# Grouped seven-product attention for layer 1, and layer 2's value projection moved behind its attention, in a six-layer graph network

## The chip, the core and the metric

The kernel runs on one NeuronCore of a Trainium2 chip. TensorE (PE) multiplies matrices, VectorE (DVE) and ScalarE (ACT) do elementwise work, GpSimd (POOL) does little here, and SyncE (SP) issues nearly all transfers. The metric is the device time of one execution in microseconds, and lower is better. All tensors that matter are float32.

## What is computed

The input is a matrix `x` of 3327 rows by 256 features and a 0/1 adjacency matrix of 3327 by 3327. Four residual layers follow one another, each `x = layernorm(x + layer(x))`. The last of them holds three graph attention layers, so the kernel counts six: "0", "1", "2", "3a", "3b", "3c". Each has masked attention over all rows:

```python
# layer 1
h = x @ W
e = leaky_relu((h @ a1)[:, None] + (h @ a2)[None, :])
att = softmax(where(adj > 0, e, -1e12), axis=1)
x = layernorm(x + elu(att @ h))
# layer 2
q, k, v = x @ Wq.T + bq, x @ Wk.T + bk, x @ Wv.T + bv
att = softmax(where(adj > 0, q @ k.T / 16, -9e15), axis=-1)
x = layernorm(x + elu(att @ v))
```

Layers 3a to 3c have the form of layer 1, with the layer norm after 3c alone. Because a row of `att` sums to one, `att @ (x @ W + b)` equals `(att @ x) @ W + b`: a projection can stand before the attention or behind it.

## The kernel before

Rows are padded to 3328, that is 26 tiles of 128 rows (`NT`) and 7 blocks (`NB`): blocks 0 to 5 have four tiles (512 query rows), block 6 has two. The main loop walks over `(L, b, j)`: layer, query block, key tile. For each step an attention weight tile `e` (128 keys by 512 queries) is made some steps ahead, and PE multiplies it with the value tile `V[L.i % 2][j]`, adding up in four PSUM banks `pos`. `V[0]` and `V[1]` take turns as a layer's input and output.

**Two ways to multiply.** In the plain way (the matmul at L1693), a step issues four matmuls of 128 by 128 by 257, the 257th column being the row sum. In the other way (`products`, L940), two key tiles make a pair, and seven products of the Strassen-Winograd kind replace eight. With 512 queries they are 14 matmuls with 128 or 129 columns to a pair, in place of 8 with 257. This needs sums of weights (`s1` to `s4`) and sums of values (`t1` to `t4`). The value sums are made once for each pair by `combine` (four DVE instructions of 128x128), stored in DRAM (`t_d`), and read back for each block by `fetch_tsum` into three buffers named `tsums`. Weight sums come from `sums` for one pair, or from `quad_sums` for a quad of four key tiles at once: there the weights lie in `QUADS`, which share their storage with `FT`.

**Who uses which.** `strassen(L, b)` says it: layer 0 in blocks 1 to 5, layer 2 in every block, 3a to 3c in blocks 0 to 5. Layer 1 is plain everywhere. Quads are used by 3a to 3c (`deep(L)`).

**`FT`** is the store of turned (transposed) feature tiles: layer 0's keys and queries, then layer 2's keys, which are layer 1's output turned. From layer 3a on nobody needs it, and it serves as `QUADS`.

**Layer 2's scores.** `pair_weights` (L638 to L678) makes the weights of two key tiles with seven products of its own (L650), from grouped keys (`ksum`, made by `sum_keys`, some kept and the others made anew in each block) and grouped queries (`gsum`). It is a generator; `products` steps it, so that score matmuls and attention matmuls lie mixed in PE's queue. Its products share two PSUM banks of three, and each is overwritten only after ACT or DVE has read what was in it.

**The end of a block** is `finish(L, b, pos)`, also a generator; the main loop advances it one step per `j` during the next block. It joins the seven products (`joined`, DVE, L972 to L984), normalises (ACT, L1188 or L1190), turns the result, projects it, applies elu, adds the residual, takes the layer norm (`bn_stats`, `rsqrt`), writes the output tile, and makes what the next layer needs. `turn` (L987) splits a block's floats into 16-bit planes (two ACT copies, L994), transposes them with one DMA (SP, L997), and joins the planes again with two copies (L1004, by DVE or ACT). In layer 1 it is done twice: for the attention's result before the projection (`projected4`, seven products, L1058, in blocks 0 to 4; L1247 in blocks 5 and 6), and for the output, into `FT[b]`. Then the value projection of layer 2 (`pv`, L1330) writes `x @ Wv + bv` into `V[0]`, and the output itself goes to DRAM (`x_d["2"]`), from where layer 2 reads it back as its residual. In layer 2 nothing is turned: the attention's result goes straight to elu.

The order of the work on an engine is not that of the source. A scheduler goes through the instructions in the source's order as a priority and issues those whose inputs and buffers are free in its own reckoning of time; each engine then runs its queue in that fixed order. Of the pools, `x4k` has two buffers (turned planes, `pT4`, `tsum`, layer 2's queries `gT`), `stage` four, `e` nine, `a` four, and the small PSUM banks three.

Of the kernel before, what the change touches and what calls it, by code (L numbers as in the profile page):

```python
# [33 lines left out]
def gnn_stack(ctx: ExitStack, tc: tile.TileContext, a: dict, N: int, out: bass.AP):  # L34
# [58 lines left out]
    for k in range(4):  # L93
# [21 lines left out]
        for k in ("0", "2", "3a", "3b", "3c")  # L115
    }
    x_d = {
        k: [dram.tile([P, D], F32, name=f"x{k}_d{t}") for t in range(NT)]
        for k in ("2", "3c")
    }  # L120
# [457 lines left out]
    def sum_queries(b):  # L578
# [23 lines left out]
        12: "w_l2_wvt",  # L602
    }

    KSTEPS = {4: 5, 6: 7, 8: 8, 11: 10, 14: 1, 16: 2, 18: 4, NT + 14: 11, NT + 16: 12}
# [99 lines left out]
    class Gat:  # L705
        def __init__(self, key):
            self.last = key == "3c"
            self.quads = ("3a", "3b", "3c").index(key) + 1 if key != "1" else 0
            self.k = w.get("k_" + key)
            self.row = w["row_" + key]  # L710
            self.sd = cols.tile([P, 2, NT], F32, tag="sd", name="sd")
            self.th = cols.tile([P, NT], F32, tag="th", name="th")
            self.rh = cols.tile([P, NT], F32, tag="rh", name="rh")
            self.nrh = cols.tile([P, NT], F32, tag="nrh", name="nrh")
            self.u = {}
# [69 lines left out]
        def weights(self, b, j):  # L785
# [9 lines left out]
            if self.quads and b < NB - 1:  # L795
                e = quad(self.quads, b, j)[:, j % 4, :]
            elif self.last and b == NB - 1:
                e = V[0][j]
            else:
                e = work.tile([P, CH], F32, tag="e", name="e", bufs=9)  # L800
# [15 lines left out]
    def strassen(L, b):  # L816
        if L.key == "0":
            return 0 < b < NB - 1
        if deep(L):
            return b < NB - 1  # L820
        return L.key == "2"

    def deep(L):
        return L.i > 2

# [5 lines left out]
    def combine(key, p, v, e=None):  # L831
# [4 lines left out]
        if (key, p) in kept or key == "0":  # L836
# [150 lines left out]
    def turn(x4, n, out, steps=3, copy=nc.vector.tensor_copy):  # L987

        half = "p k (n t) -> p t k n"
# [10 lines left out]
        trv = tr[:, : 4 * n, :].rearrange("p (k t h) i -> p t k h i", t=2, h=2)  # L1002
# [3 lines left out]

    def early(L, b):
        return deep(L) and b < NB - 2

    def turn_steps(L, b):  # L1010

        if L.key == "1":
            return 5 if b == NB - 2 else 3
# [10 lines left out]

    def sum_weights(wt):
        b11, b12, b21, b22 = (wt[:, h, o * H : (o + 1) * H] for h in range(2) for o in range(2))
        t1, t2, t3, t4 = wsum
        nc.vector.tensor_tensor(t1, b12, b11, ALU.subtract)
        nc.vector.tensor_tensor(t3, b22, b12, ALU.subtract)
        nc.vector.tensor_tensor(t2, b22, t1, ALU.subtract)  # L1030
        nc.vector.tensor_tensor(t4, t2, b21, ALU.subtract)

    def projected4(pT4, wt, c4):

        add, sub = ALU.add, ALU.subtract
        av = pT4.rearrange("p (a k) h q -> p a k h q", k=2)
        a11, a12, a21, a22 = (av[:, :, k, h, :] for k in range(2) for h in range(2))
        s3, s1, s2, s4 = (
            x[:, i, :].rearrange("p (a q) -> p a q", a=2)
            for x in two_slots("psums")  # L1040
            for i in range(2)
        )
        nc.vector.tensor_tensor(s3, a11, a21, sub)
        nc.vector.tensor_tensor(s1, a21, a22, add)
        nc.vector.tensor_tensor(s2, s1, a11, sub)
        nc.vector.tensor_tensor(s4, a12, s2, sub)
        yield
        b11, b12, b21, b22 = (wt[:, h, o * H : (o + 1) * H] for h in range(2) for o in range(2))
        t1, t2, t3, t4 = wsum
        cv = c4.rearrange("p (a k) (o f) -> p a k o f", k=2, o=2)  # L1050
        c11, c12, c21, c22 = (cv[:, :, k, o, :] for k in range(2) for o in range(2))

        def two(*pairs):

            pm = bank("pproj")
            for i, (l, r) in enumerate(pairs):
                for k in range(2):
                    nc.tensor.matmul(  # L1058
                        pm[:, (2 * i + k) * P : (2 * i + k + 1) * P],
                        l[:, k, :],  # L1060
                        r,
                        start=True,
                        stop=True,
                    )
            v = pm.rearrange("p (i a f) -> p i a f", i=2, a=2)
            return v[:, 0], v[:, 1]

        m1, m2 = two((a11, b11), (a12, b21))
        m6, m7 = two((s2, t2), (s3, t3))
        yield  # L1070
        nc.scalar.copy(c22, m1)
        nc.vector.tensor_tensor(c11, c22, m2, add)
        nc.vector.tensor_tensor(c22, c22, m6, add)
        nc.vector.tensor_tensor(c21, c22, m7, add)
        m5, m4 = two((s1, t1), (a22, t4))
        yield
        nc.vector.tensor_tensor(c12, c22, m5, add)
        nc.vector.tensor_tensor(c22, c21, m5, add)
        nc.vector.tensor_tensor(c21, c21, m4, sub)
        m3, _ = two((s4, b22))  # L1080
        yield
        nc.vector.tensor_tensor(c12, c12, m3, add)
# [23 lines left out]
    def finish(L, b, pos):  # L1106
# [76 lines left out]
        else:  # L1183
# [23 lines left out]
            if L.key in x_d:  # L1207
                x4 = work.tile([P, 4, D], F32, tag="stage", name="x4", bufs=4)
                xr = [x4[:, k, :] for k in range(4)]
                for k, t in enumerate(ts_):  # L1210
                    nc.sync.dma_start(xr[k], x_d[L.key][t])
# [5 lines left out]
            if L.key != "2":  # L1217
                pT4 = work.tile([P, 4, 2, P], F32, tag="x4k", name="pT4", bufs=2)
                yield from turn(
                    p4,  # L1220
                    n,
                    lambda t: pT4[:, :n].bitcast(U16).rearrange(
                        "p k h (i t) -> p t k h i", t=2
                    )[:, t],
                    turn_steps(L, b),
                    nc.scalar.copy if early(L, b) else nc.vector.tensor_copy,
                )
                if early(L, b):
                    yield
                    yield  # L1230
                pTs = {k: pT4[:, k] for k in range(n)}
                if L.key == "1" and b < NB - 2:
                    c4 = work.tile([P, 4, D], F32, tag="x4k", name="c4", bufs=2)
                    yield from projected4(pT4, w[L.w], c4)

            def projected(k):


                if L.key == "2":
                    src = p4[:, k, :]  # L1240
                elif L.key == "1" and b < NB - 2:
                    src = c4[:, k, :]
                else:
                    pm = bank("pproj")
                    pT = pTs.pop(k)
                    for h in range(2):
                        nc.tensor.matmul(  # L1247
                            pm[:, :D],
                            pT[:, h, :],
                            w[L.w][:, h, :],  # L1250
                            start=(h == 0),
                            stop=(h == 1),
                        )
                    src = pm[:, :D]
# [22 lines left out]
            for p in range(n + 2):  # L1277
                if p >= 2:
                    activated(p - 2)
                    if b == NB - 2 or early(L, b):  # L1280
# [7 lines left out]
        if not L.hidden:  # L1288
# [8 lines left out]
            else:  # L1297
                dsts = [nxt[t][:, :D] for t in ts_]
            for k, t in enumerate(ts_):
                nc.vector.tensor_scalar(  # L1300
                    dsts[k],
                    ys[k],
                    st[:, k, 0:1],
                    r[:, k : k + 1],
                    ALU.subtract,
                    ALU.mult,
                )
# [3 lines left out]
                elif L.key in ("1", "2"):  # L1311
                    nc.sync.dma_start(x_d["2" if L.key == "1" else "3c"][t], dsts[k])
# [4 lines left out]
            yield  # L1317
            if L.key == "1":
                yield from turn(
                    o4,  # L1320
                    n,
                    lambda t: FT[b].bitcast(U16).rearrange(
                        "p h (k i t) -> p t k h i", k=4, t=2
                    )[:, t, :n],
                    4 if b == NB - 2 else 3,
                )
                for k, t in enumerate(ts_):
                    pm = bank("pv")
                    for h in range(2):
                        nc.tensor.matmul(  # L1330
                            pm[:, :D],
                            FT[b][:, h, k * P : (k + 1) * P],
                            w["v"][:, h, :],
                            start=(h == 0),
                            stop=(h == 1),
                        )
                    nc.vector.tensor_tensor(nxt[t][:, :D], pm[:, :D], w["bv"], ALU.add)
                    if k % 2:
                        yield
                        if b < NB - 1:  # L1340
                            combine("2", t // 2, nxt)
                dsts = [nxt[t][:, :D] for t in ts_]
# [491 lines left out]
```

## Time and profile before

| | |
|---|---|
| median of 3 runs (lowest to highest) | 2261.28 us (2260.6 to 2264.51) |
| profiled execution | 2261.39 us, its span 2259.3 us |
| granted PE clock in it | 0.998 |
| PE busy | 2232.9 us (99%) |
| DVE busy | 1960.8 us (87%) |
| ACT busy | 1324.9 us (59%) |

The span is the time from the first to the last instruction; 2.1 us lie around it. "Busy" is the union of the time of an engine's instructions. A float32 matmul appears as two records on PE. From the starts of the main matmuls, layer 1's blocks begin at 467, 513, 565, 617, 669, 721 and 773 us, layer 2's at 807, 904, 988, 1072, 1156, 1239 and 1318 us, and those of 3a at 1359, 1405, 1451, 1496, 1540, 1584 and 1628 us.

### The profile page before, as it was taken

The page shows a single profiled execution, that of the slowest core. Times are in us where ns is not written, and L with a number is a line of the kernel's source. Part 1 is how long each engine was busy: PE and PEld are TensorE (multiplying, and loading weights), DVE is VectorE, ACT ScalarE, POOL GpSimd, SP SyncE. Part 2 cuts the span into 40 slices and gives each one's busy share as a digit, 9 for nine tenths or more (in the row PEclk, how much of TensorE's full clock was granted, in tenths as well). Part 3 has the DMA queues.
Part 4 walks back from the last instruction along what each step waited for, and adds up shares of the span by engine and source line. Part 5 has one row for each costly group of instructions (what it writes and reads, how often), then busy time and mean ns, then how long its engine had stood idle before and what let it go on. Part 6 is the DMA issues. An engine that isn't in the chain of part 4 may idle for free. (4 is left out here: it accounts for less than half of the span.)

```text
span 2259.3 us, 42140 instructions
## 1 busy us (share of the span) xinstructions
PE 2232.9 (99%) x15333; PEld 2026.2 (90%) x15333; DVE 1960.8 (87%) x5346; ACT 1324.9 (59%) x2259; POOL 78.6 (3%) x236
## 2 busy tenths in 40 slices
PE   9999999999999999999999999999999999999997
PEld 7788887888888879999999999999999999999997
DVE  7789999967667778988988889999898999899997
ACT  4677777775545534444454436766665765666663
POOL 0000001000000000000000000000000000000000
PEclk9999999999999999999999999999999999999999
DMA  8655665522332232223232244656535556355542
GB/s 279 197 177 171 195 193 190 177 90 68 92 82 55 68 87 78 66 92 92 57 97 76 76 143 151 157 146 167 143 114 157 152 144 169 101 168 162 153 121 56
DMA packets 191972, 291.41 MB, mean 129 GB/s; under 512 B 81054, under 2 KB 111253, under 8 KB 187157
## 3 DMA queue, kind: packets, MB, share of 16 engines
q1 hardware_dynamic: 185732, 283.22, 42.6%
q0 software_dynamic: 5760, 5.25, 1.5%
q8 instruction: 121, 1.98, 0.4%
q14 instruction: 87, 0.70, 0.1%
q10 hardware_dynamic: 272, 0.26, 0.0%
HBM read 228.21 MB, written 38.44 MB: 118 GB/s over the span
## 5 line engine op out<-in xcount | busy, mean ns | idle before, releaser
L788 ACT ACTIVATE re<-u,nrh,th 128x512 f32<-128x512 f32 (+1 forms) x728 | 534.0, 777 | 289.3 <-DVE e L801 147.1
L1693 PE MATMUL po<-v,e 128*128 128x257 f32 x1872 | 422.6, 381 | 0.7 <-ACT p L1190 0.6
L1693 PEld LDWEIGHTS po<-v,e 128*128 128x128 f32 x1872 | 352.6, 190 | 60.7 <-issue 9.8
L940 PE MATMUL po<-tsums,qsum 128*128 128x128 f32 (+1 forms) x2520 | 351.1, 275 | 0.9 <-DMA tsums<-t3b_d 0.5
L801 DVE SCALAR_TENSOR_TENSOR ft<-re,rh,mask 128x512 f32<-128x512 f32 x468 | 338.6, 742 | 1.9 <-ACT re L788 1.9
L940 PE MATMUL po<-tsums,ssum 128*128 128x128 f32 (+1 forms) x2082 | 316.9, 275 | 5.5 <-DMA tsums<-t3a_d 2.0
L940 PEld LDWEIGHTS po<-tsums,qsum 128*128 128x128 f32 x2520 | 315.4, 192 | 1.8 <-DMA tsums<-t3b_d 0.7
L940 PEld LDWEIGHTS po<-tsums,ssum 128*128 128x128 f32 x2082 | 286.6, 192 | 20.7 <-issue 5.0
L940 PE MATMUL po<-v,ft 128*128 128x129 f32 x1872 | 285.7, 275 | 1.0 <-DVE ft L801 0.9
L940 PEld LDWEIGHTS po<-v,ft 128*128 128x128 f32 x1872 | 251.6, 192 | 5.7 <-DVE ft L801 1.8
L940 PEld LDWEIGHTS po<-v,e 128*128 128x128 f32 x1196 | 170.2, 191 | 35.9 <-issue 23.7
L524 ACT ACTIVATE ex<-ps,rq 128x512 f32<-128x512 f32 (+1 forms) x183 | 118.9, 652 | 114.8 <-PE ps L511 111.9
L940 PE MATMUL po<-v,e 128*128 128x129 f32 x1196 | 183.3, 275 | 0.0
L801 DVE SCALAR_TENSOR_TENSOR e<-re,rh,mask 128x512 f32<-128x512 f32 (+1 forms) x234 | 148.3, 655 | 37.3 <-PE po L1693 22.5
L496 DVE SCALAR_TENSOR_TENSOR e<-ex,mask 128x512 f32<-128x512 f32 (+1 forms) x182 | 118.1, 649 | 61.0 <-ACT ex L673 30.6
L511 PE MATMUL ps<-ft 128*128 128x512 f32 (+1 forms) x364 | 166.9, 564 | 0.0
L525 DVE SCALAR_TENSOR_TENSOR e<-ex,mask 128x512 f32<-128x512 f32 (+1 forms) x183 | 116.6, 643 | 32.2 <-ACT ex L524 31.8
L940 PE MATMUL po<-tsums,ft 128*128 128x128 f32 x936 | 143.3, 275 | 0.0
L940 PE MATMUL po<-v,qsum 128*128 128x128 f32 x840 | 128.2, 275 | 0.0
L940 PEld LDWEIGHTS po<-tsums,ft 128*128 128x128 f32 x936 | 123.6, 192 | 0.1
L467 DVE CUSTOM_DVE_ANT_0 acc<-acc,stage 128x1024 uint16<-128x1024 uint16 (+1 forms) x168 | 108.6, 646 | 12.2 <-DMA stage<-in_adj_a 9.2
L650 PE MATMUL ps<-gsums,ksum 128*128 128x256 f32 x408 | 111.3, 380 | 0.0
(348 smaller groups left out, 3659.9 us busy)
## 6 DMA issues: line engine op xcount, KB each, us to landing
mask<-mask_d SPq DMA_DIRECT2D x30, 1664.0 KB
stage<-in_adj_a SPq DMA_DIRECT2D x78, 512.0 KB
tsums<-t_d SPq DMA_DIRECT2D x152, 256.5 KB
tsums<-t3a_d SPq DMA_DIRECT2D x77, 256.5 KB
tsums<-t3b_d SPq DMA_DIRECT2D x77, 256.5 KB
tsums<-t3c_d SPq DMA_DIRECT2D x77, 256.5 KB
mask_d<-mask SPq DMA_DIRECT2D x6, 1664.0 KB
u<-s_d SPq DMA_DIRECT2D x24, 256.0 KB
```

Of the source, the lines that this page charges most:

```text
L467: nc.vector.tensor_tensor(acc, acc, st[:, h * wd : (h + 1) * wd], ALU.add)
L496: nc.vector.scalar_tensor_tensor(e[:, :wd], t_[:, :wd], 0.0, mask(b, j), ALU.add, ALU.mult)
L511: nc.tensor.matmul(ps[:, :wd], FT[j // 4][:, 0, (j % 4) * P : (j % 4 + 1) * P], FT[b][:, 1, :wd], start=True, stop=True,)
L524: nc.scalar.activation(t_[:, c], ps[:, c], AF.Exp, scale=rq[:, j : j + 1])
L525: nc.vector.scalar_tensor_tensor(e[:, c], t_[:, c], 0.0, mask(b, j)[:, c], ALU.add, ALU.mult)
L650: nc.tensor.matmul(out, l, r, start=first, stop=True, skip_group_check=True)
L788: nc.scalar.activation(t_[:, :wd], self.u[b][:, :wd], AF.Relu, bias=self.nrh[:, j : j + 1], scale=self.th[:, j : j + 1],)
L801: nc.vector.scalar_tensor_tensor(e[:, :wd], t_[:, :wd], self.rh[:, j : j + 1], mask(b, j), ALU.add, ALU.mult,)
L940: nc.tensor.matmul(o, x, y, start=(p == 0 and g not in banks[:i]), stop=(p == NT // 2 - 1 and g not in banks[i + 1 :]),)
L1693: nc.tensor.matmul(pos[k], e[:, k * P : (k + 1) * P], V[L.i % 2][i], start=(i == 0), stop=(i == NT - 1),)
```

## The change

Layer 1 multiplies by seven products in blocks 1 to 5, with its weights in the quads of `FT`'s storage. So its turned output can't lie in `FT` while the layer runs: for blocks 0 to 4 it goes to DRAM (`tr_d`) and is fetched again in block 6 (`turned_again`), where ACT writes it to `FT`. Layer 1's value sums are made by `combine("1", ...)` in steps of layer 0's block 6 and of layer 1's blocks 0 and 1. `V[0]` now gets layer 1's output itself, by a transfer from the normalised tile, not the projected values; the output's turning and the steps behind it run in a second queue of generators (`tail`). The normalisation of layer 1 goes from DVE to ACT (`eased`). Its projection is the same for all blocks: eight matmuls at four tiles, not seven products. Layer 2's `finish` turns the attention's result and projects it with `Wv`, and DVE adds `bv`. Its residual is read from `V[0]`, and the grouped keys of pair 12 are no longer kept.

```diff
-        if L.key == "0":
+        if L.key in ("0", "1"):
             return 0 < b < NB - 1
-        if deep(L):
-            return b < NB - 1
-        return L.key == "2"
+        return L.key == "2" or b < NB - 1
...
+    def turned_again(g):
+        tr = work.tile([P, 16, P], U16, tag="stage", name="again", bufs=4)
+        nc.sync.dma_start(tr.rearrange("p k i -> p (k i)"), tr_d[g])
+        yield
+        yield
+        yield
+        for t in range(2):
+            nc.scalar.copy(ft_view(g, 4)[:, t], turned_view(tr, 4)[:, t])
+            yield
...
     def early(L, b):
-        return deep(L) and b < NB - 2
+        return L.is_gat and b < NB - 2
     def turn_steps(L, b):
-        if L.key == "1":
-            return 5 if b == NB - 2 else 3
+        if L.key == "2":
+            return 4 if b == NB - 2 else 3
+        if L.key == "1" and b == NB - 2:
+            return 5
...
+        if keep is not None:
+            nc.sync.dma_start(keep, tr.rearrange("p k i -> p (k i)"))
+            return
...
-            if L.key != "2":
-                pT4 = ...
+            on_act = early(L, b) or L.key == "2"
+            pT4 = ...
+            yield from turn(p4, n, ..., turn_steps(L, b),
+                nc.scalar.copy if on_act else nc.vector.tensor_copy)
...
                 if L.key == "2":
                     src = p4[:, k, :]
+                    nc.vector.tensor_tensor(src, pm[:, :D], w["bv"], ALU.add)
...
+                if eased:
+                    nc.scalar.activation(
+                        dsts[k], ys[k], AF.Identity, bias=nm[:, k : k + 1], scale=r[:, k : k + 1])
+                else:
+                    nc.vector.tensor_scalar(...)
...
-                    nc.sync.dma_start(x_d["2" if L.key == "1" else "3c"][t], dsts[k])
+                elif L.key == "2":
+                    nc.sync.dma_start(x_d[t], dsts[k])
+                elif L.key == "1":
+                    nc.sync.dma_start(nxt[t][:, :D], dsts[k])
...
-            if L.key == "1":
-                yield from turn(o4, n, lambda t: FT[b]..., 4 if b == NB - 2 else 3)
-                for k, t in enumerate(ts_):
-                    pm = bank("pv")
...
+            if L.key == "1":
+                tail.append(turn(o4, n, lambda t: ft_view(b, n)[:, t], 4,
+                    keep=tr_d[b] if b < NB - 2 else None))
+                tail.append(followed())
+                if b < NB - 1:
+                    return
...
-        if deep(L):
-            ahead_of += 4 if b else min(4, j // 3)
+        if deep(L) or L.key == "1" and b > 0:
+            ahead_of += 4 if b > (L.key == "1") else min(4, j // 3)
...
+        advance_tail()
...
+        if L.key == "0" and b == NB - 1 and j % 6 == 0 and 0 < j < 24:
+            combine("1", j // 6 - 1, V[1])
+        if L.key == "1" and j % 4 == 1 and j < (24, 12, 0, 0, 0, 0, 0)[b]:
+            combine("1", (3 if b == 0 else 9) + j // 4, V[1])
+        if L.key == "1" and b == NB - 1 and j > 0:
+            if j % 3 == 1 and j // 3 < NB - 2:
+                again.append(turned_again(j // 3))
```

## The prediction

> **What bounds the kernel now.** First the page's head:
>
> ```profile
> span 2259.3 us, 42140 instructions
> PE 2232.9 (99%) x15333; PEld 2026.2 (90%) x15333; DVE 1960.8 (87%) x5346; ACT 1324.9 (59%) x2259; POOL 78.6 (3%) x236
> ```
>
> PE never rests, so time is won by taking matmuls away and lost where PE is made to wait. Next, single blocks (layer 1's blocks 4 and 6, layer 2's block 2, 3a's block 0, 3c's block 3); columns are window, length, busy time of PE, weight load, DVE, ACT, POOL, then clock and DMA:
>
> ```profile
> 669.30:721.10 51.80, 51.80 (x253) 45.55 (x252) 37.39 (x96) 26.98 (x41) 1.31 (x2) 1.00 0.23 60
> 773.00:807.30 34.30, 33.56 (x139) 25.87 (x138) 22.16 (x75) 16.44 (x30) 0.42 (x1) 1.00 0.37 96
> 1071.90:1155.60 83.70, 83.70 (x558) 77.00 (x557) 72.88 (x226) 40.08 (x90) 0.20 (x2) 1.00 0.27 81
> 1358.70:1405.20 46.50, 44.41 (x377) 42.68 (x376) 45.90 (x113) 27.98 (x44) 0.41 (x2) 1.00 0.51 164
> 2083.50:2127.60 44.10, 44.10 (x383) 43.69 (x382) 42.88 (x99) 28.15 (x40) 0.00 (x0) 1.00 0.54 159
> ```
>
> Layer 1's plain block takes 51.8 us; 3c's block has the form that the change gives layer 1, takes 44.1, and still has PE full, but DVE at 42.9. At 3a's start DVE is the limit. Third, PE's timeline, layer 1 and then 3c (start, us, records):
>
> ```profile
> 679.66 2.11 PE L1693 MATMUL po<-v,e 128*128 128x257 f32 x9
> 681.61 1.05 PE L1058 MATMUL pproj<-w_l_w,pT 128*128 128x128 f32 x8
> ```
>
> ```profile
> 2102.25 1.03 PE L1247 MATMUL pproj<-w_l_w,pT 128*128 128x256 f32 x4
> 2103.11 0.83 PE L940 MATMUL po<-v,ft 128*128 128x129 f32 x6
> ...
> 2106.24 1.03 PE L1247 MATMUL pproj<-w_l_w,pT 128*128 128x256 f32 x4
> ```
>
> Nine wide records start within 1.95 us: 0.217 each, 0.433 a matmul. A pair of seven products takes 2106.24 − 2103.11 = 3.13; the eight plain matmuls take 3.47.
>
> **The sum on PE.** A new layer 1 block is 13 × 3.13 + 8 projection matmuls × 0.433 = 44.2, as 3c shows (44.10 from start to start, 2083.49 to 2127.59). Today's is 51.87 (669.26 to 721.12). Of the 7.77 less, 3.47 are the eight `pv` matmuls, which layer 2 issues again behind its attention: there each block gets 3.47 longer. What is gone is 4.30 a block (13 × 0.34 = 4.4, less 0.35 where `projected4`'s 14 narrow matmuls, 3.12, become 3.47; the rest is small change), in five blocks: **21.5 us**. Nothing can hide it or take it away while PE is full. Against the profiled 2261.4 (beside the median of 2261.3) that is 2239.9 with no new wait.
>
> [...] The trace says 0.112, half of the 0.217 at 257.
>
> **The waits that it adds.** Each is walked along the built program's queues with durations of the trace.
>
> *Layer 1, blocks 1 to 5.* DVE: 3c's 42.9, less four normalisations (0.33 apart, 1.3), plus eight `combine` instructions (0.20 apart, 1.6) and one small one: 43.4 of 44.1. That fits, with 0.7 to spare; over 44.1 it would cost its excess in four blocks. Block 1 needs a lead: the queue puts twelve weight tiles (0.67 apart, 8.0) and two quads' sums (eight of 0.60, 4.8) ahead of block 0's end, with seven `combine` (0.8 each, 5.6). That is 18.4 in the 15.3 that block 0 leaves DVE (30.6 busy of 45.9), so the second quad is 3 late; it is wanted only two pairs (6.3) later, the first at once. Three more `combine` follow in block 1. 3a's first two blocks took 46.5 and 45.8 for 44.2 later on, 4 in all. I take 1 (0 to 4). SP gets more: in its queue the fetches for the next block's pairs 1 and 2 stand behind the second turning DMA, which waits for ACT's planes of the output, and behind the store to `tr_d`, which waits for the landing, 4.3 us. A buffer of `tsums` lies one pair, 3.1, ahead. PE's waits of today (layers 1 to 3b), total, times, longest:
>
> ```profile
> PE po L940 <- DMA tsums<-t3b_d: 2.1, 2, 1.6
> PE po L940 <- DMA tsums<-t3a_d: 2.0, 3, 1.1
> ```
>
> A wait of 1.6 at four boundaries would be 6; with the planes issued about 3 ahead of the block's end most of it is covered, and I take 1 (0 to 6). The fetches, `t1` stores and `tr_d` themselves are covered at a DMA share of 0.23. POOL's sums by DMA are as in 3a.
>
> *Layer 1, block 6.* ACT's ten copies `ft<-again` take 1.28 each (below), 12.8, and the four normalisations 1.7: 16.4 becomes 30.9, while PE's content falls to 33.6 − 3.5 = 30.1. ACT's queue has eight of the ten copies ahead of `gT`, whose maximum PE's small matmul `pn` needs, and main matmuls queue behind `pn`. Walked from block 5's end on ACT: normalised at 3.9, one weight tile and the planes until 6.4, eleven weight tiles (0.49) until 11.8, eight copies and four elu (0.4) until 23.8, `gT` until 25.2; maximum and small steps 1.6, so `pn` at 26.8. PE: 14 key tiles of two matmuls (0.87) until 12.1, eight projections and two tiles until 17.3, four `pgq` (0.86) until 20.7, four tiles: it comes to `pn` at 24.2 and waits 2.6; 0.4 more for layer 2's first weights, which ACT makes late. I take 3 (0, if the copies slip between the tiles, to 7, today's idle and all of ACT's excess behind a full queue).
>
> *Layer 2.* How long turning takes, from 3b's ACT:
>
> ```profile
> 1796.16 1.98 ACT L994 COPY planes<-p 128x1024 uint16<-128x1024 uint16 x2
> 1798.04 3.64 ACT L788 ACTIVATE re<-u,nrh,th 128x512 f32<-128x512 f32 x5
> 1802.98 2.56 ACT L1004 COPY pT<-turned 128x1024 uint16<-128x1024 uint16 x2 [1.29 <-issue]
> ```
>
> The copies come 4.8 after the planes (4.3 in layer 1, whose DMA share of 0.23 is nearer to layer 2's 0.27), and ACT stood idle for the last 1.3: it takes its queue in order. In 3b the weights are made 6 tiles ahead, so PE notices nothing. Layer 2 has no such lead. Today its block start at 1071.86 shows on ACT:
>
> ```profile
> 1073.50 1.69 ACT L1190 ACTIVATE p<-p,zs 128x256 f32<-128x256 f32 x4
> 1075.10 0.40 ACT L1256 ACTIVATE elu_e<-p 128x256 f32<-128x256 f32 x1
> 1075.40 0.35 ACT L661 COPY ex<-ps 128x256 f32<-128x256 f32 x1
> ```
>
> After: normalised at 3.3, one bank copy 0.35, planes 2.0 until 5.7, landed at 10.0, first copy until 11.2, and behind it the bank copy `ex<-ps` (L667) until 11.6. PE may overwrite that bank only then, and comes to it after 28 products and 10 score matmuls: 28 × 0.223 + 10 × 0.434 = 10.6. So 1.0 a block in blocks 1 to 5 (0, if it lands as the queue assumes, to 4.4, if nothing covers it). Block 6, with single scores: 0.5 (0 to 3). The bias adds and the `combine("3a")` that now waits for layer 2's `x4k` buffers add 2 us to DVE at a block's end; DVE has 11 idle of 84, and the paired sums are ready 3.6 us or more before PE wants them: nothing. The four projections take a PSUM bank each; the nearest rows, `pgq` and `pn` between the same products, made PE wait 0.1 at most. Together 5.5 (0 to 25).
>
> *Elsewhere.* Layer 0's block 6 gets three `combine` (2.4 on DVE, 27 busy of 33.6): nothing. In 3a's block 0 DVE binds, at 45.9; two more bias adds make it 46.6, while layer 2's last projection (1.7) moves there and fits into PE's 2.1 idle: −0.9 (−1.7 to 1). The residual's reloads disappear from SP; they delayed nobody.
>
> Sum: −21.5 + 1 + 1 + 3 + 5.5 − 0.9 = −11.9: **2249.5 us**.
>
> **Rivals.**
> *All hidden* (17%): the queues were laid out with these waits in view, and 3c's blocks run at 97% on DVE without loss. 2239 to 2244.
> *Layer 2 and SP at twice my price* (17%): landing at 4.8, joins later by the extra `combine`, fetches late at four boundaries: −21.5 + 1 + 6 + 4 + 8 = −2.5, so 2259; 2254 to 2263.
> *ACT's wait for the turned planes exposed in layer 2* (11%), the one that ends slower: if nothing useful stands between planes and copy, a block loses landing and both copies, 4.4 + 2.6 = 7.0, six times 42: 2261.4 − 21.5 + 4 + 42 = 2286. With 4 us for the other waits it eats the gain at 2.9 a block, and is measurably slower at 3.7. For it: PE's queue has no slack there. Against: five ACT operations, some 2.8 us busy, stand between, and PE works on meanwhile.
>
> **How the numbers follow.** The main case (55%) is 2244 to 2254: half to one and a half of the 9.6 us of waits. About 0.2% (4.5 us) is what a measurement can tell. Faster: 55 + 17 and a quarter of the second rival, 76%; same: the rest of it, 13%; slower 11%. Range: 2238 (no wait, and 3a's start wins 1.7) to 2263, the second rival's end.
>
> **What would show it.** Layer 1's blocks 2 to 5 at 44 to 45 and DVE at 43 to 44 in them; layer 2's blocks 1 to 5 at 88.2 (83.7 + 3.5 + 1.0), PE waiting there for a bank behind ACT's `pT` copy; layer 1's block 6 at 33, with `pn` late. Wrong if layer 1's blocks exceed 46 (DVE or `tsums`), or layer 2's exceed 90.

## The result, and the profile after

The changed kernel takes 2286.05 us (median of four runs, 2282.35 to 2291.43); the kernel before took 2260.94 beside it. The ratio is 1.011, 95% interval 1.0086 to 1.0133: slower by 1.1%, where 0.5% faster was forecast, and outside the range. The profiled execution, the slowest of the four, took 2291.43 us, 5.4 over the median; the accounts below are made on it.

Head of its page:

```profile
span 2289.4 us, 43944 instructions
...
PE 2230.4 (97%) x16053; PEld 2043.5 (89%) x16053; DVE 2015.9 (88%) x5466; ACT 1383.1 (60%) x2333; POOL 91.5 (4%) x269
```

PE is busy as long as before, with fewer matmul columns, and now rests 59 us. Single blocks, in the columns of the prediction (window, length, PE, weight load, DVE, ACT, POOL, clock, DMA share): layer 1's blocks 1 to 5, and layer 2's block 2.

```profile
514.30:558.40 44.10, 44.10 (x381) 43.66 (x380) 36.56 (x86) 26.58 (x40) 1.47 (x4) 1.00 0.61 153
558.40:609.20 50.80, 46.57 (x383) 45.50 (x382) 44.27 (x111) 31.13 (x46) 3.64 (x6) 0.97 0.64 170
609.20:660.50 51.30, 47.40 (x383) 46.66 (x382) 43.40 (x104) 31.05 (x46) 3.64 (x6) 0.93 0.70 173
660.50:707.00 46.50, 44.62 (x383) 43.85 (x382) 42.13 (x97) 30.95 (x46) 3.66 (x6) 1.00 0.61 161
707.00:759.70 52.70, 47.70 (x382) 46.73 (x381) 39.98 (x103) 28.26 (x45) 3.65 (x6) 0.94 0.71 159
980.40:1069.90 89.50, 87.60 (x575) 80.01 (x574) 76.48 (x234) 43.95 (x94) 0.20 (x2) 1.00 0.28 76
```

Block 1 of layer 1 takes 44.10 us with PE full: the sum on PE was right. The blocks after it, with the same matmuls, take 50.8, 51.3, 46.5 and 52.8 us. Below, a block's *content* is the time that PE needs for its matmuls without waits, here 44.2 us. Two columns changed that the prediction had not priced: the granted clock, 0.93 and 0.94 in blocks 3 and 5, and the DMA share, 0.61 to 0.71 where it was 0.23 in block 4 before. The share alone doesn't make a block slow: block 1 has 0.61 too.

PE's waits from layer 1's block 1 to its end (total, times, longest), and VectorE's longest kind of wait there:

```profile
PE po L939 <- DVE p L981: 3.7, 2, 3.3
PE po L939 <- DMA tsums<-t_d: 3.7, 3, 1.6
PE po L939 <- DVE p L979: 2.7, 1, 2.7
PE po L939 <- issue: 2.7, 1, 2.7
PE po L939 <- DVE tsum L851: 2.2, 1, 2.2
PE pproj L1200 <- DVE y L1218: 1.9, 1, 1.9
PE pproj L1200 <- DVE pT L1011: 1.2, 1, 1.2
PE pn L562 <- DVE g L559: 0.8, 1, 0.8
```

```profile
DVE tsum L844 <- DMA turned<-planes: 13.1, 5, 5.4
```

The start of block 3 on VectorE, on SyncE and on PE shows how one leads to the other (start, us, what, and the idle time before it):

```profile
609.75 0.41 DVE L980 TENSOR_TENSOR p<-p,po 128x256 f32<-128x256 f32 x1
613.68 0.29 DVE L844 TENSOR_TENSOR tsum<-v 128x128 f32<-128x128 f32 x1 [3.51 <-DMA turned<-planes]
...
614.29 0.41 DVE L981 TENSOR_TENSOR p<-p,po 128x256 f32<-128x256 f32 x1
```

```profile
606.27 4.24 SPq L1001 DMA_TRANSPOSE turned<-planes  x1
...
613.67 0.32 SPq L1007 DMA_DIRECT2D tr_d<-turned  x1
```

```profile
614.85 1.20 PE L939 MATMUL po<-tsums,ft 128*128 128x128 f32 x4 [3.25 <-DVE p L981]
...
617.98 1.92 PE L939 MATMUL po<-tsums,qsum 128*128 128x128 f32 x8
619.69 0.64 PE L939 MATMUL po<-v,ft 128*128 128x129 f32 x2
...
622.44 1.06 PE L939 MATMUL po<-tsums,qsum 128*128 128x128 f32 x8
623.33 0.39 PE L939 MATMUL po<-v,ft 128*128 128x129 f32 x2
```

`combine("2")` for the second pair writes a buffer of `x4k`. Of its two buffers one still holds `planes`, which the turning DMA of the block's output reads until 613.67, 7.4 us after its issue (before the change the output's turning was read 4.3 to 5.5 us after it). VectorE takes its queue in order, and the join at L981, which would free a PSUM bank, stands behind it. PE waits 3.3 us. And then PE is slow: eight records from 617.98 take 1.71 to the next start, the same eight from 622.44 take 0.89. The granted clock agrees (same columns):

```profile
609.20:615.00 5.80, 2.55 (x23) 2.38 (x22) 2.29 (x10) 0.00 (x0) 0.86 (x1) 0.91 1.17 235
615.00:620.00 5.00, 5.00 (x24) 5.00 (x25) 5.00 (x10) 4.73 (x8) 1.82 (x3) 0.50 0.80 217
```

After the stall the clock is halved: it is 0.50 in 613.93:620.75, as it is for 3.4 us behind the stalls at the starts of blocks 2 and 5, in 562.73:566.14 and 712.91:716.33. In blocks 2 to 5 together, counted from start to start of PE's records, stalls of over half a microsecond come to 16.2 us, and matmuls at double pitch lose some 7.5 more; these blocks are 24.5 over their content of 4 × 44.2.

In layer 2, ScalarE and PE in block 2:

```profile
991.40 1.33 ACT L1011 COPY pT<-turned 128x1024 uint16<-128x1024 uint16 x1 [2.12 <-DMA turned<-planes]
992.60 0.36 ACT L664 COPY ex<-ps 128x256 f32<-128x256 f32 x1
```

```profile
990.49 0.61 PE L939 MATMUL po<-v,ssum 128*128 128x128 f32 x4
993.01 0.70 PE L647 MATMUL ps<-gsums,ft 128*128 128x256 f32 x2 [1.90 <-ACT ex L664]
```

This is the wait that the prediction walked to: PE needs the bank, its copy at L664 stands behind the first `pT` copy, which waits for the turning DMA.

### The profile page after: what moved, and what is told of

It is laid out like the page before. It is cut to its first block, busy times and chain, and to the rows that moved or that the text cites. A ratio compares the mean times of both kernels' runs of the same rounds, so it can differ in the third digit from the quotient of the medians.

```text
span 2289.4 us, 43944 instructions
## 1 busy us (share of the span) xinstructions
PE 2230.4 (97%) x16053; PEld 2043.5 (89%) x16053; DVE 2015.9 (88%) x5466; ACT 1383.1 (60%) x2333; POOL 91.5 (4%) x269
## 5 line engine op out<-in xcount | busy, mean ns | idle before, releaser
L939 PE MATMUL po<-tsums,qsum 128*128 128x128 f32 (+1 forms) x3240 | 455.8, 277 | 9.6 <-issue 2.7
L799 DVE SCALAR_TENSOR_TENSOR ft<-re,rh,mask 128x512 f32<-128x512 f32 x598 | 433.6, 742 | 16.6 <-ACT re L786 15.0
L939 PEld LDWEIGHTS po<-tsums,qsum 128*128 128x128 f32 x3240 | 409.5, 193 | 11.8 <-issue 4.5
L939 PE MATMUL po<-v,ft 128*128 128x129 f32 x2392 | 368.2, 277 | 3.4 <-DVE p L979 2.7
L939 PEld LDWEIGHTS po<-v,ft 128*128 128x128 f32 x2392 | 323.9, 193 | 8.6 <-issue 3.1
L939 PEld LDWEIGHTS po<-v,e 128*128 128x128 f32 x1196 | 169.3, 191 | 35.6 <-issue 23.2
L1675 PE MATMUL po<-v,e 128*128 128x257 f32 x832 | 192.5, 382 | 0.6 <-DVE e L523 0.6
L939 PE MATMUL po<-tsums,ft 128*128 128x128 f32 x1196 | 185.3, 278 | 3.7 <-DVE p L981 3.7
L1675 PEld LDWEIGHTS po<-v,e 128*128 128x128 f32 x832 | 156.8, 191 | 32.1 <-issue 9.1
L939 PE MATMUL po<-v,qsum 128*128 128x128 f32 x1080 | 166.0, 277 | 0.0
L939 PEld LDWEIGHTS po<-v,qsum 128*128 128x128 f32 x1080 | 143.7, 194 | 0.1
```

The lines of the kernel that those rows point to most:

```text
L799: nc.vector.scalar_tensor_tensor(e[:, :wd], t_[:, :wd], self.rh[:, j : j + 1], mask(b, j), ALU.add, ALU.mult,)
L939: nc.tensor.matmul(o, x, y, start=(p == 0 and g not in banks[:i]), stop=(p == NT // 2 - 1 and g not in banks[i + 1 :]),)
L1675: nc.tensor.matmul(pos[k], e[:, k * P : (k + 1) * P], V[L.i % 2][i], start=(i == 0), stop=(i == NT - 1),)
```

## The experiments

All are edits of the changed kernel, or sums of them (e12 is the kernel before once more); its median is 2286.05. In brackets stands the ratio to the kernel before, with its 95% interval. Block times are from each one's profiled execution; layer 1's blocks 2 to 5 sum to 201.3 us in the changed kernel, for a content of 176.8.

**Where VectorE's wait comes from: e1, e2.** In e1 the second combine is moved behind the joining; in e2 it gets a buffer of another pool.

```diff
                     if L.key == "1" and b < NB - 1:
+                        if k:
+                            for _ in range(4):
+                                yield
                         combine("2", (ts_[0] + k) // 2, nxt)
```

> One edit of the changed kernel: in layer 1's second queue of generators, four more steps pass before the second pair's combine for layer 2, so that VectorE's queue holds it behind the joining of the next block's products and not ahead of it. Theory A (in-order wait on a shared buffer: that combine writes a buffer of x4k that the planes of the output still hold until the turning DMA has read them, VectorE stands in it for up to 5.4 us, the joining stands behind it, PE cannot reuse its banks, and its clock then falls to half for some 3.4 us): the PE waits of 2.8, 3.4 and 2.9 us at the starts of layer 1's blocks 2, 3 and 5 go, with their slow stretches; these blocks fall from 50.8, 51.3 and 52.8 to 45 to 47 us, and the kernel from 2286 to 2270 to 2276. Theory B (VectorE has too much work in layer 1, 43.4 us of 44.1): the joining stays late, the blocks stay above 50, 2283 to 2290. Theory C (fetches of value sums late in SyncE's queue): waits of PE for tsums stay, and no block falls below 50.

```diff
+        elif key == "2":
+            t = work.tile([P, 4 * H + 1], F32, tag="stage", name="tsum", bufs=4)
         else:
             t = work.tile([P, 4 * H + 1], F32, tag="x4k", name="tsum", bufs=2)
```

> One edit of the changed kernel: the value sums that layer 1 makes for layer 2 are written to a buffer of the pool stage (four buffers) in place of x4k (two); the order stays near the old one. Theory A (wait on the planes' buffer): VectorE's waits behind the turning DMA (13.1 us at five boundaries) fall below 3 us, blocks 2, 3 and 5 to 45 to 47, the kernel to 2270 to 2276, unless stage is held as long. Theory B (too much work on VectorE) and theory C (SyncE's queue): no block falls below 50, 2283 to 2290.

e1: 2280.5 us (ratio to before 1.0085, 1.007 to 1.010). e2: 2273.9 (1.0052, 1.0037 to 1.0067). In e2 VectorE waits no more for the turning DMA in a `tsum`; blocks 2 to 5 sum to 190.2, block 3 falls from 51.3 to 46.4 and block 5 from 52.8 to 48.3, but block 2, for which theory A gave 45 to 47, stays at 51.2: PE's waits for `tsums` in layer 1 have grown from 3.7 to 7.0 us, the longest 3.1. In e1 they are 10.6 us, block 2 stays at 51.0, and the four sum to 192.8; a part is given back, as block 6 grows from 42.3 to 47.0, where `pT` waits 6.6 us for a turning DMA that comes late. So theory A holds with 8 to 11 us of the 24.5; theory B, VectorE too full, does not explain these; and the fetches (C) have a share.

**The accumulating DMAs: e3, e13.** The changed kernel has one more line, which the section on the change doesn't show: layer 1's column sums (`xsum`, for the next layer's row of means) are no longer added by VectorE but by 20 transfers of 128 KB on GpSimd's queue that add to what lies at their destination. e3 takes this line back.

```diff
-                L.sum = Sum(L.is_gat)
+                L.sum = Sum(deep(L))
```

> One edit of the changed kernel: layer 1's column sums are added by VectorE as before the change, not by GpSimd's accumulating DMAs. Theory D (GpSimd's queue: the one-column memset of a value sum stands behind accumulating DMAs that wait for each other and for the stored output; the store of the sums, and behind it on SyncE the fetches, then come late): PE's waits for tsums in layer 1 (3.7 us, and 2.2 at the end of block 5) go with their slow stretches, 2276 to 2281, less some 1 us a block for four more adds on VectorE. Theory A (VectorE's wait on the planes' buffer): little changes, 2284 to 2292. Theory B (VectorE too full): slower, by 0.6 to 1.3 us a block, 2289 to 2293.

2272.2 us (1.0055, 1.0034 to 1.0076): blocks 2 to 5 at 47.6, 48.0, 44.9 and 47.3, in sum 187.7. Theory A had expected no change here and was too narrow; D has the direction, but its gain was to be 5 to 10 us, and 13.8 came. VectorE still waits in `tsum`, and PE still has a stall about as long as those of the changed kernel, but this one isn't followed by a slow stretch (start and clock rows):

```profile
DVE tsum L844 <- DMA turned<-planes: 8.5, 6, 3.1
```

```profile
611.16 0.68 PE L939 MATMUL po<-tsums,ft 128*128 128x128 f32 x4 [2.73 <-DVE p L981]
```

```profile
611.20:614.60 3.40, 3.40 (x31) 3.40 (x32) 3.40 (x8) 3.01 (x6) 0.00 (x0) 1.00 0.92 248
```

In blocks 2 to 5 stalls fall from 16.2 to 9.7 us and the slow stretches go, so about half of the gain there is the clock's. For which reason do the stalls fall? In e13 the accumulating DMAs stay, and only the column of ones is written by VectorE for layer 2's sums, so that nothing of them waits in GpSimd's queue.

> One edit of the changed kernel: the column of ones in layer 2's value sums is written by VectorE, not by GpSimd; the accumulating DMAs of layer 1's column sums stay. It tells why e3 gained 14 us. Theory D1 (GpSimd's queue: the ones wait behind accumulating DMAs, SyncE stands up to 6.0 us before the sums' store, and fetches behind it come late): nearly all of e3's gain comes here too, 2272 to 2276, and SyncE's waits for GpSimd go. Theory D2 (the accumulating DMAs load the DMA engines, and the turning DMA, on which VectorE waits, takes 5.7 to 7.4 us for 4.3): little gain, 2281 to 2288, the turning DMA as slow as before.

2280.8 us (1.0083, 1.0066 to 1.010). SyncE's waits for GpSimd, 15.9 us before, are gone, but blocks 2 to 5 still sum to 198.7 (49.8, 54.3, 44.1 and 50.5) and four stalls of 2.4 to 4.4 us are there. That lies at the lower edge of theory D2's range: GpSimd's queue is the smaller part, some 5 us, and the larger one goes with the accumulating DMAs themselves. Turning the attention's result in these blocks takes 5.7 to 8.8 us from issue to first reader in the changed kernel, 5.5 to 8.6 in e13, and 4.6 to 5.3 in e3. The output's turning, for which VectorE stands in `tsum`, changes less: from issue to the store behind it 5.7 to 7.4 us, 5.1 to 8.2, and 4.7 to 7.2. That the transfers slow each other by sharing the DMA engines is inferred from this, not shown; the mean DMA share hardly tells these kernels apart (0.60 to 0.64 in e3's blocks, 0.61 to 0.71 in the changed kernel's).

**Both: e5.**

> The edits of e2 and e3 together: layer 2's value sums in a buffer of stage, and layer 1's column sums on VectorE. Theory A+D (two causes: VectorE waits for the planes' buffer, and the accumulating DMAs make the turning DMA and the fetches slower): both gains add up in part: layer 1's blocks 2 to 5 at 44.5 to 46, 8 to 12 us below e3's 187.7 for the four, total 2260 to 2266. Theory of one cause (the accumulating DMAs alone, by slowing the turning DMA that VectorE waits for): no more than e3, 2270 to 2274. Theory B (VectorE too full): slower than e3, since VectorE has the adds and no cover.

2264.7 us (1.0017, 1.0008 to 1.0026), in the range of theory A+D. Blocks 3 and 4:

```profile
603.70:649.40 45.70, 44.68 (x382) 43.90 (x381) 44.24 (x109) 31.47 (x46) 0.20 (x2) 1.00 0.65 177
649.40:694.00 44.60, 44.48 (x383) 43.86 (x381) 44.17 (x106) 30.96 (x46) 0.20 (x2) 1.00 0.63 158
```

The four blocks sum to 181.4, 6.3 below e3 where 8 to 12 were expected. No stall in them is longer than 1.1 us, and the clock is 1.00 throughout: with the stalls the slow stretches went too. The DMA share is as high as in the changed kernel. VectorE is now busy for 44.2 us in blocks 3 and 4; that it sets what is left isn't shown, since block 5 takes 45.7 us with VectorE at 40.7.

**Half of the change: e4.** Layer 1 plain again, all else as changed.

```diff
-        if L.key in ("0", "1"):
+        if L.key == "1":
+            return False
+        if L.key == "0":
             return 0 < b < NB - 1
...
-        if L.key == "0" and b == NB - 1 and j % 6 == 0 and 0 < j < 24:
+        if False:
             combine("1", j // 6 - 1, V[1])
...
```

(The quads, the other sums of values and the longer lead of layer 1 go with it.)

> Half of the change: layer 1 multiplies plainly in all blocks again, the rest stays (value projection behind layer 2's attention, turned rows by way of DRAM, second queue, accumulating DMAs). PE's content is that of before plus 1.7 us (eight projection matmuls in place of the seven products of four tiles). Layer 2's blocks should stay at 88 to 90 and layer 1's block 6 with layer 2's block 0 at 132 together: these parts cost 15 to 17 us over their content in the changed kernel. Theory A (the combine's wait on the planes' buffer) puts waits at the starts of layer 1's blocks here too: blocks at 50 to 54 for a content of 48.5, total 2284 to 2300. Theory B (VectorE too full with grouped weights): none, blocks at 48.5, total 2276 to 2281.

2290.4 us (1.0133, 1.0116 to 1.0150). Layer 1's blocks 2 to 5 take 49.1 to 50.2 us for 48.5: theory A expected 50 to 54 and missed for the blocks, though the total is in its range. In a plain block VectorE is busy for only 28 of 48 us, and of its waits in `tsum` for the turning DMA two are left, 4.7 us in all; that the idle time covers them is a reading, not shown. Layer 1's block 6 with layer 2's block 0 takes 132.1, layer 2's blocks 1 to 6 488.2. So without the seven products the kernel is 28 us slower than before, and they, worth 22 us on PE, win back about 4, which the two intervals don't tell apart from nothing.

**Layer 2: e6.**

```diff
-            on_act = early(L, b) or L.key == "2"
+            on_act = early(L, b)
```

> One edit of the changed kernel: in layer 2 the two copies that join the turned planes go from ScalarE to VectorE. Theory E (ScalarE takes its queue in order: the bank copy at L664 stands behind the first of these copies, which waits for the turning DMA, and PE waits for the bank 0.9 to 2.1 us in each of blocks 1 to 5): these waits go, layer 2's blocks 1 to 5 fall from 88.4, 89.5, 88.4, 89.7 and 84.1 to 87.3 (blocks 1 to 4) and 82.1, together 7 to 9 us, total 2277 to 2280. Rival F (the wait only moves: VectorE stands in its own queue behind the turning DMA, and weight sums and bank adds stand behind that): layer 2 gains less than 3 us or loses up to 10, total 2283 to 2296.

2274.9 us (1.007, 1.0053 to 1.0087). Layer 2's blocks 1 to 5 take 87.3, 87.4, 87.3, 87.7 and 82.5 us, with PE full in block 3:

```profile
1062.10:1149.40 87.30, 87.30 (x575) 79.89 (x574) 77.05 (x236) 41.95 (x92) 0.20 (x2) 1.00 0.28 77
```

Theory E is confirmed: layer 2 falls from 576.6 to 567.0 us, and in layer 2 nothing that PE needs at once stood behind the same wait on VectorE. A small part comes back one layer later: 3a's block 1 takes 47.5 to 50.4 us in the five kernels with this edit (e6, e9, e10, e11, e14) and 45.6 to 46.6 in all others.

**Layer 1's block 6: e8.** Every second copy `ft<-again` on VectorE.

```diff
-            nc.scalar.copy(ft_view(g, 4)[:, t], turned_view(tr, 4)[:, t])
+            (nc.vector.tensor_copy if t else nc.scalar.copy)(
+                ft_view(g, 4)[:, t], turned_view(tr, 4)[:, t]
+            )
```

> One edit of the changed kernel: of the ten copies that put layer 1's turned rows into FT in its block 6, five go from ScalarE to VectorE. Theory I (ScalarE's copies of 1.3 us hold up elu and gT, and PE waits for a bank and for the norms there: 2.0, 0.4 and 1.0 us): block 6 and layer 2's block 0 together fall from 132.3 to 129 to 130.5, total 2282 to 2285. Rival J (the late turning of block 5's result sets the end of block 6, whatever ScalarE does; VectorE, 30 us busy of 42, then comes late with weights): 132 or more, total 2285 to 2292.

2280.6 us (1.0088, 1.0073 to 1.0103). Block 6 and layer 2's block 0 together fall from 132.3 to 129.3, inside theory I; the total is better than its 2282 to 2285. PE's wait at `pn` stays at 0.7 us (0.8), so the copies had not set it. And 3 us is no more than other edits move here: e2, with ScalarE's copies as they were, has 128.9.

**Layers 3a to 3c: e7, e12, e14.** Their code is the same, and they took 900.6 us before and 910.8 after. e7 lays the new DRAM tiles behind the old ones.

```diff
-        for k in ("0", "1", "2", "3a", "3b", "3c")
+        for k in ("0", "2", "3a", "3b", "3c", "1")
```

> One edit of the changed kernel: the DRAM tiles of layer 1's value sums are laid behind those of the other layers, so that the value sums of layers 2 to 3c lie at the addresses that they had before the change. The instructions are the same. Theory G (layers 3a to 3c, whose code is the same, take 907 to 911 us in all profiled executions of changed kernels for 900.6 before because their fetches come from other addresses): 3a to 3c at 900 to 902, total 2276 to 2280. Theory H (addresses do not matter; the fetches' waits come from elsewhere or vary from run to run): 3a to 3c at 906 to 911, total 2282 to 2290.

2284.3 us (1.0102, 1.0087 to 1.0117), with 905.5 in these layers: the addresses of the value sums explain at most a part.

> The kernel before, profiled once more, for layers 3a to 3c, which took 900.6 us in its profile and 903 to 911 in those of the changed kernels with the same code. Theory H (the fetches' waits there differ from run to run): 900 to 908 here, with other waits for tsums than the first time, and the difference of 10 us to the changed kernel's profile is mostly such variation. Theory K (the change slows them): 900 to 901 again, with the same waits.

The kernel before gives 898.3 us this time (2259.57 in all). All profiles of changed kernels lie at 903.1 to 910.8, so theory H alone doesn't hold: something of 3 to 12 us reaches layers that were not touched. The order of the work isn't it in 3b and 3c: in all changed kernels but e14, every engine's queue holds the same instructions in the same order from 3b's start on as before, and these two layers take 604.8 to 613.7 us for 602.8 and 604.1. The waits for `tsums<-t3b_d`, in the second profile of before and in e9 below:

```profile
PE po L940 <- DMA tsums<-t3b_d: 1.1, 2, 0.6
```

```profile
PE po L941 <- DMA tsums<-t3b_d: 3.1, 3, 1.2
```

**Together: e9, e10, e11, e14.** e9 has the edits of e2, e3, e6 and e8.

> The edits of e2, e3, e6 and e8 together in the changed kernel. If the four waits are separate: e5's 2264.7, less 8 to 9.5 us in layer 2's blocks 1 to 6 (e6's 434.5 + ... as there: layer 2 at 567 for 576), less 2 to 3 us in layer 1's block 6 and layer 2's block 0, is 2252 to 2256, 0.2 to 0.4% faster than the kernel before; the rest over the content of 2240 is VectorE in layer 1's blocks (44.2 us busy of 44.6 to 45.7), block 6, and fetches in 3a to 3c. If the waits replace each other (a VectorE that now has the column sums, the turned copies of layer 2 and half of the copies of block 6 comes late somewhere else): 2260 to 2268.

2254.4 us (0.9969, 0.9958 to 0.9980): the waits were separate, and this version is faster than the kernel before by 0.3%.

```profile
PE 2216.9 (99%) x16053; PEld 2033.1 (90%) x16053; DVE 2030.5 (90%) x5505; ACT 1363.4 (61%) x2314; POOL 73.3 (3%) x249
```

PE makes as many matmuls as in the changed kernel in 13.5 us less busy time; in layer 1's blocks the slow stretches are gone.

> As e9, and layer 2's value sums are made from the normalised tile itself, ahead of its turning, not from the stored output behind it: VectorE need not wait for the transfer that writes V (4.7 us of waits in e5, 4.4 and 2.7 in e2). If that wait still ends anything: layer 1's blocks 2 to 5 fall from 45.4 to 44.2 to 44.8, total 2 to 5 us below e9. If VectorE's work alone sets these blocks (44.2 busy), no change within 2 us; if the turned tile now waits for a buffer of stage, up to 6 us more.

2253.3 us (0.9967, 0.9954 to 0.9979): no difference to e9. Blocks 2 to 5 of layer 1 sum to 181.6 for e9's 182.2; the wait for the stored output ended nothing.

> As e9, and layer 1's transfers v<-o and the stores to tr_d are issued by GpSimd, which has nothing else to do there, in place of SyncE, so that the fetches of value sums no longer stand behind them. Theory C (SyncE's order makes fetches late at the block boundaries; PE's waits for tsums are 2.4 us in e5): these waits go, 1 to 4 us below e9. Rival (the transfers' own time and the crowded DMA engines make them late, whoever issues them): within 1.5 us of e9, or up to 5 slower if GpSimd's issue is slow.

2258.6 us (0.9985, 0.9976 to 0.9994): 4 us slower than e9, as the rival had it at its worse end. In its profile PE's waits for `tsums<-t_d` fall from 1.9 to 0.5 us, but 2.4 us come up that the profile puts down to nothing, blocks 2 to 5 stay at 182.0, and block 6 grows from 39.5 to 42.8. So these stores' places in SyncE's queue were worth nothing; what else stands there ahead of a fetch, the turning DMA and the stores to `t_d`, was not moved.

e14 is e9 without any accumulating DMAs (`Sum(False)`).

> As e9, and in layers 3a to 3c too VectorE adds the column sums, so that no accumulating DMA is left there. It tells why these layers' fetches come late. Theory M (the accumulating DMAs share the engines with the fetches of value sums and make some of them late): 3a to 3c lose their waits for tsums (6 to 7 us in e9) and take 900 to 903 us for e9's 905.8, unless VectorE, 42 to 43 us busy of 44.2, is overfilled by four adds a block (1.3 us): then up to 1 us more in each of 15 blocks. Theory N (the waits come from the masks' transfers and the order on SyncE): the waits stay, and the time is e9's or up to 15 us above it.

2252.8 us (0.9962, 0.9949 to 0.9975), no different from e9 within their intervals. The waits for `t3b_d` fall from 3.1 to 0.7 us, as theory M says, those for `t3a_d` stay (2.8, now 2.9), and 3a to 3c take 907.5 us for 905.8: 3a's block 1 takes 50.4 (49.8 in e9), with the clock at 0.93, and block 2 grows from 45.5 to 47.6, where VectorE is busy for 46.6. Why these layers lose time in every changed kernel stays open.

## Why the prediction was wrong, step by step

The profiled span is 42 us over the one forecast (2289.4 for 2247.4).

- **The sum on PE**, −21.5: right. Layer 1's block 1 takes 44.10 for 44.2, and e9 lies 15 us above the forecast without waits of 2239.9, with the waits that are left in it. The rate that it counted on, 0.112 us for a record of 128 or 129 columns, is block 1's too: a pair's 28 records take 3.13 us there, from 529.95 to the next start at 533.08.
- **Layer 1, blocks 1 to 5**, +1 and +1, bounds 0 to 4 and 0 to 6: here lies most of the error, 22.4 us (245.4 us measured in the five blocks). Two steps failed.
  - **"That fits, with 0.7 to spare"**: VectorE's load was foreseen well (43.4; measured 40.0 to 44.3 in blocks 2 to 5), but its order was not walked. The prediction looked for `x4k` in layer 2 only, not at `combine("2")` in layer 1, which stands ahead of the joining and waits for the buffer of `planes`: a wait put at nothing, for which VectorE stood 13.1 us. Without it the kernel is 12.1 us faster (e2).
  - **"POOL's sums by DMA are as in 3a"**, and with it **"The fetches, `t1` stores and `tr_d` themselves are covered at a DMA share of 0.23"**: put at nothing too. 0.23 was the lowest share of the five blocks before (0.23 to 0.32); the change itself raises it to 0.61 to 0.71, and turning, priced at 4.3 us, took 5.7 to 8.8. Not the share but the accumulating DMAs make the difference that the runs show: without them the kernel is 13.8 us faster (e3), or 9.2 on top of e2 (e5), at nearly the same share. In 3a to 3c they cost nothing that e14 could show, so "as in 3a" was no guide to layer 1. How they slow the rest stays open.
  - Both edits together (e5) win 21.4 of the 36.6 us between the forecast and the median. What was predicted instead, fetches late on SyncE, is there too: PE's three waits for `tsums` sum to 3.7 us.
- **The clock**: not in the sum at all. It made 16.2 us of stalls in blocks 2 to 5 into 23.7, out of the 24.5.
- **Layer 1, block 6**, +3 (0 to 7): in the range, but only in part for its reason. With layer 2's block 0 it is 6.1 over its content (132.3; before 131.4, less 5.2 of `pv`). PE waited 0.8 us at `pn`, not 2.6, and longer at the projection, 1.9 for VectorE's `y` and 1.2 for `pT`. ScalarE's copies may have 3.0 of the 6.1 (e8).
- **Layer 2**, +5.5 (0 to 25): mechanism, place and bank right, price doubled: blocks 1 to 6 are 11.4 over their content. Blocks 1 and 3 lost 1.2 us, near the 1.0 forecast; in blocks 2 and 4 the turning landed a microsecond later, and PE's wait alone was 1.9. Blocks 5 and 6 had 2.0 and 2.3 over their content, for 1.0 and 0.5.
- **3a's block 0**, −0.9 (−1.7 to 1): right in sign, 46.05 us for 46.50, half the size. 3a as a whole takes 297.2 for 296.5. For 3b and 3c nothing was put down; they cost 9.6 in this execution, more than in any other (604.8 us in e6, 613.7 here).

Of the rivals, the one that ended slower named 2286 us, the time that was measured, by luck: it had 42 us in layer 2, where 11.4 were found. "Layer 2 and SP at twice my price" came nearest for layer 2 and had no room for layer 1. The stated sign, layer 1's blocks over 46 by DVE or `tsums`, came true.

## What to carry to other kernels

Walk every instruction that a moved step puts into an in-order queue back to the buffer that it writes, and ask who holds that buffer and for how long; spare busy time on the engine does not cover a wait that stands ahead of what PE needs next (here VectorE was busy for 43.4 of block 3's 51.3 us, and PE waited 3.3). Where the change adds transfers, don't carry a transfer's duration over from the stage before it: here 4.3 us became 5.7 to 8.8. And where PE is full otherwise, put a term for the clock beside each long stall: here 16.2 us of stalls cost some 7.5 more.

## What the runs showed of the hardware

- In all profiled executions, after their first 100 us, PE had twenty stalls of 2.6 us or more before a matmul of 128 or more columns (2.64 to 6.80, from start to start of its records, less the usual distance). Behind seventeen of them records of 128 columns soon started 0.21 us apart in place of 0.11, for 2.6 to 5.8 us, and such a stretch lost 1.2 to 2.8 us. Behind three (2.89 in e3, 3.12 in e7, 2.68 in e11) the clock stayed at 1.00. After stalls of 1.4 to 2.5 us it happened in some cases and not in others (in the changed kernel behind one of three stalls of 2.1 us). In the changed kernel's profile the granted clock was 0.50 for 3.4, 6.8 and 3.4 us behind the stalls of 2.8, 3.4 and 2.9 us at the starts of blocks 2, 3 and 5, and for 3.4 us (757.29:760.70) behind one of 2.3 us.
- In layer 1's blocks 1 to 5 a turning DMA of one block was first read, or stored, 4.3 to 4.7 us after its issue, once 5.5, in the kernel before (DMA share 0.23 to 0.32), and 5.7 to 8.8 in the changed kernel (0.61 to 0.71); it held SyncE's queue for 2.3 to 4.7 us where it had been 1.5 to 2.7. The share is not the rule: in e3, at 0.60 to 0.64, the attention's result was read after 4.6 to 5.3 us in blocks 2 to 5.
